# Moving four first loads to ScalarE's queue, narrower idle products, ScalarE for a copy, and a later start of a small task, in a four-layer graph network on one core

## The chip, the cores and the metric

The kernel runs on one core of a Trainium2 chip. The core has TensorE (PE in the profile; its weight loads are shown as PEld), VectorE (DVE), ScalarE (ACT), GpSimd (POOL) and SyncE (SP). SyncE issues nearly all transfers from memory. A queue carries out its instructions in order, so an instruction that waits holds all behind it. The metric is the device time of one execution in microseconds (us), as the median of several runs.

## The reference

The input is x, 3327 nodes by 64 features, and adj, a weighted and nearly empty 3327 by 3327 adjacency matrix. Four layers follow one another, each on a layer-normalised input clipped at zero, and each added to x:

```
h = max(layernorm(x), 0)
layer 0: two gated cells:  m = adj @ (h @ W);  h = relu(GRU(m, h))     # x += h
layer 1: w = decayed weights by the rank of a nonzero among the last 100 of its row
         x += w @ (h @ weight) + bias
layer 2: three hops with adj*adj:  h = (adj*adj @ h) @ W.T + b         # x += h
layer 3: two hops:  h = tanh(concat[adj @ h, h] @ W[k])                # x += h
```

In one cell, `r = sigmoid(i_r + h_r)`, `z = sigmoid(i_z + h_z)`, `n = tanh(i_n + r*h_n)` and the new h is `(1-z)*n + z*h`, where the three i come from m and the three h from the old h. So adj is multiplied eight times by a 64-column matrix, and everything else is small beside that.

## The kernel before

**Tiling.** The nodes are padded to 26 blocks of 128, laid out as 13 pairs of blocks. The 13 pairs form four chunks of 3, 3, 3 and 4 pairs (384, 384, 384 and 512 columns for each of the two halves), and two groups: group 0 holds chunks 0 and 1, group 1 chunks 2 and 3. A tile is one block of 128 sources against all columns of one group: 768 KB for group 0 and 896 KB for group 1. Tiles live in 20 slots. `Tile.load` (line 409) takes the slot that has been free longest and issues the transfer on SyncE's queue (line 412).

**Products.** There are eight products with adj, k = 0 to 7: 0 and 1 are the two cells, 2 is the ranked layer, 3 to 5 are the squared hops, 6 and 7 the last layer. `alone` and `joint` (lines 646 and 662) write a list of units (k, chunk, tile). A `joint` stage uses each tile for two products, k and k+1, one group at a time, so that the tile is loaded once. Beside product 0 a counting product (line 549) is made of a 0/1 mask of each tile, which VectorE writes (line 473). It gives the number of nonzeros behind each block, kept in `totals`. In product 2, masks (line 473 on 127 rows, the last row brought by a GpSimd transfer of `totals`, line 478) are multiplied by a triangle of constants (called from line 517, shown under line 314), and ScalarE or VectorE turn the sums into the bits of a weight e (lines 530 and 528). Then TensorE multiplies e by the features (line 614).

**Order of the work.** The order on every engine is fixed when the program is written: `run` (line 718) walks the list of units, up to 44 units ahead with loads, 24 with masks and 3 with the expansion to e. All other work stands in tasks, which are Python generators. A task yields a number of planned microseconds. `spend` (line 381) takes a planned price for each unit from every task's number and lets those tasks go on whose number has run out. `later_task(us, task)` starts a task after so many planned microseconds from the start of `run`. `finish` makes a task go to its end where its result is needed.

**What is touched.**

- `load_x` (line 118) and lines 1043 to 1051: before `run`, x is loaded in three parts and four tiles between them, all on SyncE's queue: x part 0, tile, x part 1, tile, tile, rest of x, tile. `load_cell(0)` then loads the first cell's weights and all biases (lines 154 and 157) into `stage`, which GpSimd has set to zero before (line 1043).
- `warm_up` (line 172) makes 14 products (28 instructions) of x with itself that nobody reads, 384 columns each, ahead of the first true product.
- `before_0` makes the layer norm of a chunk (lines 841 to 856), whose result y is the first product's input, and transposes it (line 798; copies at line 800).
- `evacuate_stacked` (line 830) copies a product's sums out: the upper half on ScalarE (line 831), the lower half on VectorE (line 832). `gru` (line 872) calls it for both cells and goes on with the gates (line 883), the sigmoids (line 888), two VectorE steps (lines 893 and 895), tanh (line 904) and the blend (lines 908 to 915).
- `last_sources(g)` (line 565) prepares the last row of every block as sources of the ranked layer, as one extra unit: GpSimd clears half a slot (line 571), SyncE loads two small parts (line 575), VectorE makes two steps (lines 577 and 581) and ScalarE one (line 583). Its result `lastw` is used by the last unit of each chunk in product 2. For group 0 it starts at planned time 130, for group 1 at 155 (line 1062).

Of the kernel before, what the change touches and what calls it, by code (L numbers as in the profile page):

```python
# [44 lines left out]
N, D = 3327, 64  # L45
P = 128
NB = 13
# [4 lines left out]
CH = [(0, 3), (3, 6), (6, 9), (9, 13), (3, 5), (5, 6)]  # L52
NC = 4
# [11 lines left out]
W1, IH1, HH1, W2, IH2, HH2 = 0, 1, 4, 7, 8, 11  # L65
# [26 lines left out]
def upper(n):  # L92
    return slice(n * D, (n + 1) * D)
# [3 lines left out]
def kernel(  # L97
# [9 lines left out]
    nc = tc.nc  # L107
# [7 lines left out]


    xs = const.tile([P, NB, 2, D], F32, name="xs")
    def load_x(g0, g1):
        nc.sync.dma_start(out=xs[:, g0:g1], in_=x[:, g0:g1])

    load_x(*CH[0])
    slots = [const.tile([P, 2, GWM], F32, name=f"adj{i}") for i in range(NBUF)]
    mhalf = const.tile([P, 8], F32, name="mhalf")
    nc.gpsimd.memset(mhalf, -0.5)
# [3 lines left out]
    stage = const.tile([P, 7 * D + NBIAS], F32, name="stage")  # L128
    w3 = const.tile([P, 2, 2, D], F32, name="w3")
    both = [const.tile([P, 2, (b1 - b0) * P], F32, name=f"both{c}") for c, (b0, b1) in enumerate(CH[:NC])]  # L130
# [20 lines left out]
                            compare_op=ALU.is_gt, fill=0.0, base=2 - P, channel_multiplier=1)  # L151

    def load_cell(cell):
        nc.sync.dma_start(out=stage[upper(0), :7 * D].rearrange("p (w f) -> p w f", f=D),
                          in_=weights[:, (W1, W2)[cell]:(W1, W2)[cell] + 7])
        if cell == 0:
            nc.sync.dma_start(out=stage[upper(0), 7 * D:], in_=bias_cols)

    def unfold_cell(cell):

# [11 lines left out]
    def warm_up():  # L172

        i, ps = take()
        for n in range(7):
            for h in range(2):
                nc.tensor.matmul(ps[upper(h), :width(0)], xs[:, 0, h, :], flat(xchunk(0)), start=True, stop=True)
        give(i)

    def fold_cell(cell):  # L180
# [67 lines left out]
    def more_constants():  # L248
# [32 lines left out]
        for c in range(NC):  # L281
            yield 4.0
            ahead_of_cell(c)
        yield 47.0
        load_cell(1)
        yield 20.0
        unfold_cell(1)
# [15 lines left out]
    def blocks(c):  # L303
        return CH[c][1] - CH[c][0]

    def width(c):
        return blocks(c) * P
# [15 lines left out]
    def take(sums=False, either=True):  # L323


        either = either and not sums
        pool = idle_sums if sums else idle_temps
        if either and idle_sums and (not pool or released[idle_sums[0]] < released[pool[0]]):
            pool = idle_sums
        for c in list(tasks):  # L330
            if not pool and c not in running:
                advance(c)
        i = pool.popleft()
        return i, banks[i]

    def give(i):
        released[i] = max(released) + 1
        (idle_sums if i < 4 else idle_temps).append(i)
# [5 lines left out]
    def flat(t):  # L344
        return t.rearrange("p b s d -> p b (s d)")
# [4 lines left out]
    def xchunk(c):  # L350
        return xs[:, CH[c][0]:CH[c][1]]
# [8 lines left out]
    def advance(c):  # L360
        running.add(c)
        try:
            tasks[c][1] = next(tasks[c][0])
        except StopIteration:
            del tasks[c]
        running.discard(c)

    def begin(c, task):
        finish(c)
        tasks[c] = [task, 0.0]  # L370
        advance(c)

    def finish(c):
        while c in tasks:
            advance(c)

    def later_task(us, task):
        yield us
        yield from task
# [185 lines left out]
    def last_sources(g):  # L565

        w = sum(width(c) for c in GROUPS[g])
        w0 = CH[GROUPS[g][0]][0] * P
        room = Mask(w)
        v = room.view.rearrange("p s w -> p (s w)").bitcast(F32)  # L570
        nc.gpsimd.memset(v, 0.0)  # L571
        yield 4.0
        rows = adjT.rearrange("(q p) (s n) -> q p s n", p=P, s=2)
        for s in range(2):
            nc.sync.dma_start(out=v[s * D:s * D + NQ], in_=rows[:, P - 1, s, w0:w0 + w])
        yield 12.0
        nc.vector.tensor_scalar(v, v, 0.0, 129.0 * TWO7, op0=ALU.not_equal, op1=ALU.mult)
        for c in GROUPS[g]:
            finish(("count", c))
        yield 1.0  # L580
        nc.vector.scalar_tensor_tensor(v, totals[g], -TWO7, v, op0=ALU.mult, op1=ALU.add)
        yield 1.5
        nc.scalar.activation(lastw[g], v, AF.Relu, bias=bitsb)
        room.free()
# [37 lines left out]
    units = []  # L622
# [204 lines left out]
                yield 1.2  # L827
        return yk

    def evacuate_stacked(acc, c):  # L830
        nc.scalar.copy(both[c][upper(0), 0], acc[0][1][upper(0), :width(c)])  # L831
        nc.vector.tensor_copy(both[c][upper(1), 1], acc[1][1][upper(1), :width(c)])  # L832
        for i in {acc[0][0], acc[1][0]}:
            give(i)

# [36 lines left out]
    def gru(acc, c, bi, bh, cell, pace=1.0):  # L872

        w = width(c)
        evacuate_stacked(acc, c)
        yield 0.8 * pace
        at = dead.popleft()
        r, z, d = (slots[at].rearrange("p s w -> p (s w)")[:, i * CWM:i * CWM + w] for i in range(3))

        def gate(g):  # L880
            i, ps = take()
            for s in range(2):
                nc.tensor.matmul(ps[upper(1 - s), :w], cells[:, cell, s, g, :], both[c][:, s], start=True, stop=True)
            return i, ps

        for g, v in enumerate((r, z)):
            i, ps = gate(g)
            nc.scalar.activation(v, ps[:, :w], AF.Sigmoid, bias=bsum[:, cell, g:g + 1])
            give(i)
        nh = None if cell == 0 else gate(2)  # L890
        ni = gate(3)
        yield 1.0 * pace
        nc.vector.scalar_tensor_tensor(r, ahead[c] if nh is None else nh[1][:, :w], bcol[:, bh + 2:bh + 3], r,
                                       op0=ALU.add, op1=ALU.mult)
        nc.vector.tensor_tensor(r, r, ni[1][:, :w], ALU.add)
        give(ni[0])
        if nh is not None:
            give(nh[0])
        else:
            del ahead[c]  # L900
            if not any(ch in ahead for ch in GROUPS[c // 2]):
                rooms[c // 2].free()
        yield 1.0 * pace
        nc.scalar.activation(r, r, AF.Tanh, bias=bcol[:, bi + 2:bi + 3])
        yield 0.8 * pace
        for s in range(2):
            u = upper(1 - s)
            nc.vector.tensor_tensor(d[u], both[c][u, s], r[u], ALU.subtract)
        nc.vector.tensor_tensor(d, d, z, ALU.mult)
        nc.vector.tensor_tensor(d, d, r, ALU.add)  # L910
        if cell == 0:
            nc.vector.tensor_scalar(both[c][upper(0), 1], d[upper(0)], 0.0, None, op0=ALU.max)
        yield 2.4 * pace
        if cell == 0:
            nc.scalar.activation(both[c][upper(1), 0], d[upper(1)], AF.Relu)
            yield 1.0 * pace
        return at, d
# [27 lines left out]
    def after_0(c, acc):  # L945
        at, _ = yield from gru(acc, c, BI1, BH1, 0)
        dead.append(at)
        i, v = stacked_to_nodes(c, lambda s: ident[:, upper(1 - s)])
        yield 0.8
        yk = nodes(c)  # L950
        nc.vector.tensor_copy(flat(yk), v)
        give(i)
        y[1][c] = yk

    def after_1(c, acc):
        pace = 1.0 if c in GROUPS[0] else 1.2
        at, h2T = yield from gru(acc, c, BI2, BH2, 1, pace)
        v = transpose_to_nodes(h2T, c)
        dead.append(at)
        yield 0.8 * pace  # L960
        residual(v, c, relu=True)
        yk = nodes(c)
        yield from layernorm_relu(yk, c, TWO27, 1.2 * pace, squares_on_scalar=c in GROUPS[1])
        y[2][c] = yield from in_three(yk, c)
        yield 80.0 if c in GROUPS[1] else 14.0
        add_row(c, 3)
# [40 lines left out]
    def after_6(c, acc):  # L1007
        evacuate_stacked(acc, c)
        yield 1.3
        v = stacked_to_nodes(c, lambda s: w3[:, 0, s])  # L1010
        yk = nodes(c)
        nc.scalar.activation(flat(yk), v[1], AF.Tanh)
        give(v[0])
        y[7][c] = yk
        yield 8.0
        yield from transpose_on_vector(yk, c)
# [24 lines left out]
    alone(0, 7, sweep=6, parts=True)  # L1041

    nc.gpsimd.memset(stage, 0.0)
    first = list(dict.fromkeys(t for _, _, t in units))[:4]
    first[0].load()
    load_x(*CH[1])
    first[1].load()
    first[2].load()
    load_x(CH[2][0], NB)
    first[3].load()  # L1050
    load_cell(0)
    warm_up()
    for c in (0, 0, 0, 1, 0, 1, 1):
        if c in tasks:
# [4 lines left out]
    begin(2, later_task(4.0, before_0(2)))  # L1059
    begin(3, later_task(10.0, before_0(3)))  # L1060
    begin(NC + 1, later_task(130.0, last_sources(0)))
    begin(NC + 2, later_task(155.0, last_sources(1)))
    run()
    for c in list(tasks):
        finish(c)
# [39 lines left out]
```

## Time and profile before

| | us |
|---|---|
| median of 3 runs (703.73 to 704.52) | 703.85 |
| the profiled execution's own time | 704.14 |
| its span, first to last instruction | 702.2 |
| busy: TensorE | 684.9 |
| busy: weight loads, beside TensorE's products | 378.0 |
| busy: VectorE | 348.8 |
| busy: ScalarE | 271.9 |
| busy: GpSimd | 80.5 |

201 MB are moved, 287 GB/s over the span. A line of the timeline gives start, duration, engine, line of the kernel, operation, output and inputs with their shape, and, where an engine had stood before, how long and for whom in brackets. Products in four-byte numbers appear as two instructions each.

### The profile page before, as it was taken

The numbers are of one execution on the slowest core, as the hardware profiler recorded it, in microseconds if no ns is written. First come the engines' busy times: TensorE is split into PE (matmuls) and PEld (weight loads), VectorE is DVE, ScalarE is ACT, GpSimd is POOL, SyncE is SP. The second block draws the span as 40 slices with busy tenths as digits, with TensorE's granted clock in tenths as the row PEclk, the third lists the DMA queues.
The fourth block names the chain that finished last, engine by engine and source line by source line (L and its number), as shares of the span: only waits on it lengthen the run. The fifth ranks groups of instructions, "written<-read, shape, count | busy, mean of one in ns | idle before, by whom it ended". The sixth has DMA issues, their size and how long they took to land.

```text
span 702.2 us, 12670 instructions
## 1 busy us (share of the span) xinstructions
PE 684.9 (98%) x5128; PEld 378.0 (54%) x5128; DVE 348.8 (50%) x746; ACT 271.9 (39%) x422; POOL 80.5 (11%) x114
## 2 busy tenths in 40 slices
PE   7998999999999999999999999999999999999997
PEld 3684667744566686446444444333444444344586
DVE  4945835733997889747533106425271565005101
ACT  1112100212146878888998206832166600000101
POOL 5300000002284233011100000000000000000000
PEclk9999999999999999999999999999999999999999
DMA  8999998089776943683799659963998399917991
GB/s 312 401 402 404 406 406 278 1 295 401 252 240 257 385 162 101 235 290 100 268 386 347 237 179 408 405 250 122 385 366 270 107 398 405 406 73 273 403 403 49
DMA packets 68693, 201.31 MB, mean 287 GB/s; under 512 B 7244, under 2 KB 8372, under 8 KB 68636
## 3 DMA queue, kind: packets, MB, share of 16 engines
q1 hardware_dynamic: 65740, 199.46, 76.3%
q8 instruction: 40, 0.66, 0.4%
q10 hardware_dynamic: 720, 0.85, 0.3%
q0 software_dynamic: 2176, 0.20, 0.2%
q14 instruction: 17, 0.14, 0.1%
HBM read 199.45 MB, written 0.85 MB: 285 GB/s over the span
## 4 chain that ended last, share of the span: by engine, by line
PE 58%; DVE 1%; ACT 0%; POOL 0%; issue 0%; ACTq 0%; DVEq 0%; POOLq 0%
PE sum L614 54%; PE temp L314 3%; PE temp L781 1%; POOL st L852 0%; DVE xs L1026 0%; ACT t L1023 0%; DVE both L832 0%; ACT both L831 0%; DVE e L528 0%; ACTq L1028 0%; PE sum L314 0%; DVE y L848 0%; DVE t L843 0%; DVE y L856 0%; DVE st L849 0%
## 5 line engine op out<-in xcount | busy, mean ns | idle before, releaser
L614 PE MATMUL sum<-adj,y 128*64 128x384 f32 (+3 forms) x3016 | 535.8, 501 | 3.7 <-DMA adj<-in_adjT 2.5
L614 PEld LDWEIGHTS sum<-adj,y 128*64 128x64 f32 x3016 | 247.0, 137 | 233.8 <-issue 193.9
L447 ACT ACTIVATE adj<-adj 128x768 f32<-128x768 f32 (+1 forms) x176 | 144.2, 891 | 45.2 <-PE sum L614 22.8
L473 DVE TENSOR_SCALAR adj<-adj 128x768 bf16<-128x768 f32 (+3 forms) x208 | 113.5, 597 | 32.6 <-PE temp L549 24.7
L614 PE MATMUL sum<-e,both 128*64 128x384 bf16 (+1 forms) x624 | 73.9, 339 | 0.5 <-DVE e L528 0.5
L530 ACT ACTIVATE e<-temp,bitsb 128x384 int16<-128x384 f32 (+1 forms) x120 | 67.5, 608 | 14.4 <-PE temp L314 8.1
L831 ACT COPY both<-sum 64x384 f32<-64x384 f32 (+3 forms) x17 | 8.1, 478 | 151.2 <-PE sum L614 150.1
L832 DVE COPY both<-sum 64x384 f32<-64x384 f32 (+3 forms) x17 | 9.6, 568 | 109.7 <-ACT both L831 109.7
L852 POOL TENSOR_TENSOR st<-st,mhalf 128x6 f32<-128x6 f32 (+1 forms) x16 | 24.8, 1553 | 288.3 <-DVE st L850 288.3
L449 DVE TENSOR_TENSOR adj<-adj 128x768 f32<-128x768 f32 (+1 forms) x32 | 30.6, 1005 | 52.0 <-DMA adj<-in_adjT 33.3
L314 PE MATMUL temp<-adj,tri 128*64 128x384 bf16 (+1 forms) x332 | 51.4, 341 | 1.3 <-DVE e L528 1.2
L614 PEld LDWEIGHTS <-both 128*64 128x64 bf16 x624 | 41.2, 110 | 19.0 <-issue 6.5
L528 DVE TENSOR_SCALAR e<-temp 128x384 int16<-128x384 f32 (+1 forms) x46 | 28.3, 617 | 20.8 <-ACT e L530 10.9
L314 PEld LDWEIGHTS <-tri 128*64 128x64 bf16 x416 | 28.9, 110 | 17.4 <-issue 9.0
L478 POOL DMA_DIRECT2D adj<-totals x52 | 31.5, 607 | 51.6 <-PE temp L314 44.6
L810 DVE STREAM_TRANSPOSE both<-y 32x96 f32<-32x96 f32 (+1 forms) x128 | 35.6, 278 | 2.9
L549 PE MATMUL temp<-adj,behind 128*64 128x384 bf16 x208 | 33.7, 340 | 2.8 <-DVE adj L473 2.8
L826 DVE STREAM_TRANSPOSE y<-t 32x96 f32<-32x96 f32 (+1 forms) x64 | 17.8, 278 | 25.4 <-ACT t L817 24.5
L549 PEld LDWEIGHTS <-behind 128*64 128x64 bf16 x208 | 20.3, 110 | 16.6 <-issue 13.0
L762 DVE COPY t<-sum 128x384 f32<-128x384 f32 x6 | 3.3, 555 | 34.9 <-PE sum L614 34.9
L187 ACT COPY t<-temp 128x128 f32<-128x128 f32 x1 | 0.3, 266 | 48.2 <-PE temp L185 48.2
L571 POOL MEMSET adj<- 128x768 f32 (+1 forms) x2 | 1.9, 950 | 137.6 <-PE sum L614 137.6
(130 smaller groups left out, 353.3 us busy)
## 6 DMA issues: line engine op xcount, KB each, us to landing
adj<-in_adjT SPq DMA_DIRECT2D x130, 768.0 KB, 8.9
adj<-in_adjT SPq DMA_DIRECT2D x104, 896.0 KB, 12.1
xs<-in_x SPq DMA_DIRECT2D x1, 448.0 KB
adj<-totals POOLq DMA_DIRECT2D x26, 3.0 KB, 5.0
adj<-totals POOLq DMA_DIRECT2D x26, 3.5 KB, 3.2
xs<-in_x SPq DMA_DIRECT2D x2, 192.0 KB, 2.5
out<-xs ACTq DMA_DIRECT2D x2, 192.0 KB
out<-xs ACTq DMA_DIRECT2D x1, 256.0 KB
```

The lines of the kernel that those rows point to most:

```text
L314: nc.tensor.matmul(out[hs], lhsT[:, hs], rhs, start=start, stop=stop)
L447: nc.scalar.activation(sq, v, AF.Square)
L449: nc.vector.tensor_tensor(sq, v, v, ALU.mult)
L473: nc.vector.tensor_scalar(t.mask.view[:rows, half], t.view()[:rows, half], 0.0, None, op0=ALU.not_equal)
L478: nc.gpsimd.dma_start(out=t.mask.view[P - 1:P], in_=totals[t.g][t.q:t.q + D + 1:D, :])
L528: nc.vector.tensor_scalar(wide[:, s], ps[:, :w], BITS, 0.0, op0=ALU.add, op1=ALU.max)
L530: nc.scalar.activation(wide[:, s], ps[:, :w], AF.Relu, bias=bitsb)
L549: nc.tensor.matmul(counts[c][1][s * D:(s + 1) * D, :w], behind[:, NQ - 1 - t.q:NQ - 1 - t.q + D], t.mask.view[:, s, t.cols(c)], start=firs ...
L614: nc.tensor.matmul(acc[h][1][h * D:(h + 1) * D, :w], yq[h], rhs[h], start=first and n == 0, stop=last and n == len(terms) - 1)
L810: nc.vector.transpose(to[at:at + 32, :, q], h[q * 32:(q + 1) * 32, :, s, f * 32:(f + 1) * 32])
L826: nc.vector.transpose(yk[q * 32:(q + 1) * 32, :, s, f * 32:(f + 1) * 32], v[at:at + 32, :, q])
L852: nc.gpsimd.tensor_tensor(st[:, 3, :n], st[:, 2, :n], mhalf[:, :n], ALU.pow)
```

## The change

The rest of x, and the first cell's weights and the biases, are issued on ScalarE's queue; the four tiles are no longer loaded ahead of `run`, which loads them first thing. The idle products have 192 columns. In the first cell, both copies of the sums are ScalarE's. Group 1's last sources start at planned time 200.

```diff
-    def load_x(g0, g1):
-        nc.sync.dma_start(out=xs[:, g0:g1], in_=x[:, g0:g1])
-
-    load_x(*CH[0])
+    for queue, (g0, g1) in ((nc.sync, CH[0]), (nc.scalar, CH[1]), (nc.scalar, (CH[2][0], NB))):
+        queue.dma_start(out=xs[:, g0:g1], in_=x[:, g0:g1])
...
     def load_cell(cell):
-        nc.sync.dma_start(out=stage[upper(0), :7 * D].rearrange("p (w f) -> p w f", f=D),
-                          in_=weights[:, (W1, W2)[cell]:(W1, W2)[cell] + 7])
+        queue = nc.sync if cell else nc.scalar
+        queue.dma_start(out=stage[upper(0), :7 * D].rearrange("p (w f) -> p w f", f=D),
+                        in_=weights[:, (W1, W2)[cell]:(W1, W2)[cell] + 7])
         if cell == 0:
-            nc.sync.dma_start(out=stage[upper(0), 7 * D:], in_=bias_cols)
+            queue.dma_start(out=stage[upper(0), 7 * D:], in_=bias_cols)
...
-                nc.tensor.matmul(ps[upper(h), :width(0)], xs[:, 0, h, :], flat(xchunk(0)), start=True, stop=True)
+                nc.tensor.matmul(ps[upper(h), :3 * D], xs[:, 0, h, :], xs[:, 0:3, 0], start=True, stop=True)
...
-    def evacuate_stacked(acc, c):
+    def evacuate_stacked(acc, c, on_scalar=False):
         nc.scalar.copy(both[c][upper(0), 0], acc[0][1][upper(0), :width(c)])
-        nc.vector.tensor_copy(both[c][upper(1), 1], acc[1][1][upper(1), :width(c)])
+        if on_scalar:
+            nc.scalar.copy(both[c][upper(1), 1], acc[1][1][upper(1), :width(c)])
+        else:
+            nc.vector.tensor_copy(both[c][upper(1), 1], acc[1][1][upper(1), :width(c)])
...
-        evacuate_stacked(acc, c)
+        evacuate_stacked(acc, c, on_scalar=cell == 0)
...
     nc.gpsimd.memset(stage, 0.0)
-    first = list(dict.fromkeys(t for _, _, t in units))[:4]
-    first[0].load()
-    load_x(*CH[1])
-    first[1].load()
-    first[2].load()
-    load_x(CH[2][0], NB)
-    first[3].load()
     load_cell(0)
...
-    begin(NC + 2, later_task(155.0, last_sources(1)))
+    begin(NC + 2, later_task(200.0, last_sources(1)))
```

## The prediction

> **What bounds the kernel now.** I read the page's totals, then the half-microsecond windows of the start, then the order of time around every place where TensorE (PE) stands.
>
> ```profile
> PE 684.9 (98%) x5128; PEld 378.0 (54%) x5128; DVE 348.8 (50%) x746; ACT 271.9 (39%) x422; POOL 80.5 (11%) x114
> ```
>
> PE is busy 684.9 of 702.2 us, so only its 17.3 idle us can be won. By windows they lie in 0 to 40 us (3.4 before the first product, then 1.6, 1.0 and 0.3), 40 to 60 (0.5), 60 to 80 (2.2), 220 to 240 (1.6), 260 to 300 (1.4), and at the end, which the change doesn't touch.
>
> The start, in windows of 0.5 us; columns: stretch, length, busy of PE, PEld, DVE, ACT, POOL, clock, DMA share, GB/s:
>
> ```profile
> 2.00:2.50 0.50, 0.00 (x0) 0.00 (x0) 0.00 (x0) 0.09 (x1) 0.40 (x1) 1.00 0.78 221
> 2.50:3.00 0.50, 0.00 (x0) 0.00 (x0) 0.00 (x0) 0.00 (x0) 0.00 (x0) 1.00 0.78 151
> 3.00:3.50 0.50, 0.14 (x2) 0.14 (x4) 0.16 (x1) 0.00 (x0) 0.00 (x0) 1.00 0.50 68
> 3.50:4.00 0.50, 0.50 (x2) 0.15 (x4) 0.47 (x2) 0.00 (x0) 0.00 (x0) 1.00 0.66 209
> 4.00:4.50 0.50, 0.50 (x4) 0.24 (x2) 0.47 (x2) 0.00 (x0) 0.00 (x0) 1.00 0.98 393
> ```
>
> From 4 us the DMA engines are full, at 390 to 406 GB/s, until after 100 us; before that there is a hole. In the first stage PE needs 1.6 us for a tile (8 products of 0.16, 4 counting ones of 0.08) and a 786 KB tile takes 1.94 us, so PE, late at first, catches up at 54.9 us and then waits for tiles. The last one lets it go at 60.77. Timeline from there; columns: start, length, engine, line, what, idle before:
>
> ```profile
> 60.77 0.87 PE L614 MATMUL sum<-adj,y 128*64 128x384 f32 x4 [0.75 <-DMA adj<-in_adjT]
> ...
> 65.65 0.47 ACT L831 COPY both<-sum 64x384 f32<-64x384 f32 x1 [0.72 <-PE sum L614]
> 66.16 0.56 DVE L832 COPY both<-sum 64x384 f32<-64x384 f32 x1 [1.88 <-ACT both L831]
> 66.75 0.56 DVE L473 TENSOR_SCALAR adj<-adj 128x768 bf16<-128x768 f32 x1
> 67.22 0.61 DVE L893 SCALAR_TENSOR_TENSOR adj<-adj,bcol,adj 128x384 f32<-128x384 f32 x1
> 67.36 0.32 PE L549 MATMUL temp<-adj,behind 128*64 128x384 bf16 x1 [0.95 <-DVE adj L473]
> ```
>
> VectorE stands 1.88 us at L832 because ScalarE copies first; the mask L473 is queued behind it, and PE waits 0.95 us for that mask. From 80 us on PE is the bound, so what is won earlier stays won. VectorE then holds PE twice; first where group 1's last sources are prepared now (VectorE, then PE):
>
> ```profile
> 230.48 0.55 DVE L528 TENSOR_SCALAR e<-sum 128x384 int16<-128x384 f32 x1
> 230.95 1.08 DVE L581 SCALAR_TENSOR_TENSOR adj<-totals,adj 128x896 f32<-128x896 bf16 x1
> 231.95 0.55 DVE L848 TENSOR_TENSOR y<-t 128x384 f32<-128x384 f32 x1
> 232.53 0.55 DVE L849 TENSOR_REDUCE st<-y 128x6 f32<-128x384 f32 x1
> 233.12 0.17 DVE L850 TENSOR_SCALAR st<-st 128x6 f32<-128x6 f32 x1
> 233.20 0.56 DVE L528 TENSOR_SCALAR e<-temp 128x384 int16<-128x384 f32 x1
> ```
>
> ```profile
> 233.81 0.82 PE L314 MATMUL temp<-adj,tri 128*64 128x384 bf16 x4 [0.91 <-DVE e L528]
> ```
>
> PE waits 0.91 us for an L528 that has L581 ahead of it. And second, where they would go (PE, then VectorE):
>
> ```profile
> 280.62 0.65 PE L614 MATMUL sum<-e,both 128*64 128x384 bf16 x5 [0.46 <-DVE e L528]
> ```
>
> ```profile
> 280.03 0.54 DVE L528 TENSOR_SCALAR e<-temp 128x384 int16<-128x384 f32 x1
> 280.50 0.61 DVE L473 TENSOR_SCALAR adj<-adj 127x896 bf16<-127x896 f32 x1
> 281.03 0.68 DVE L528 TENSOR_SCALAR e<-sum 128x512 int16<-128x512 f32 x1
> ```
>
> VectorE has no gap between 262 and 285 us, and PE uses each e as soon as it is written.
>
> **What the Trainium skill says.** "DMA: Bandwidth & Descriptors", section "Issuing engines are not separate DMA queues": transfers started by ScalarE and SyncE run on the same 16 engines and only the issue time is saved. Section "Queues, rings and completion order" adds that each engine goes round between the queues packet by packet, so x and the first tile will share. No transfer of before is on ScalarE's queue at the start, so the trace can't confirm it; the hole shows what issue time can be worth. "TensorE: Matmul & The Clock Gate", part 1: full clock after about 3.4 us of activity, half again after an idle window as long. The trace agrees roughly: pairs of idle products start 0.64 us apart until 6.5 us, 3.1 us after the first, then 0.32. "ScalarE: Activation LUTs", "What ACT_TABLE_LOAD costs": some 1.28 us; the trace has 1.28.
>
> **The change, part by part.**
>
> *Loads.* Four issues leave SyncE's queue between the tiles (0.59, 0.70, 0.64, 0.95 us) and four go to ScalarE's, where only a table load and, from 12.9 us, the copies L800 stand behind. Weights and bias wait there for the memset of stage, done at 2.4 us; delayed table load: free, 1.28 us must fit before 12.9, and four issues of 2.9 us after 0.8 end near 4. The bytes ahead of the last tile stay the same, so only the hole counts. Between 2 and 4 us 324 KB moved; at the 402 GB/s of the next us it would be 805, a lack of 481 KB or 1.2 us. The 640 KB of x now issued from 0.8 us can fill part, but the first x transfer, alike in shape, got at most 221 GB/s. I take 0.8 us won; ends 0.2 lost (x's first part arrives later by sharing) and 1.2 won. VectorE's reduction of chunk 1, which stood 1.47 us for x at 7.54 with chunk 0's last step behind it, runs at once, and y is ready near 8.1 instead of 9.4. That alone wins nothing: PE then stands longer for tile 3, at 15.75 now behind the same bytes.
>
> *Idle products.* 28 instructions, 6.28 us, with 192 for 384 columns: half the time each, ending near 7.4. Nothing, since y at 8.1 covers it; if the clock fell, the clock rival pays.
>
> *Copies of cell 0.* Chunk 0: two copies on ScalarE take 0.97 us (L800's pair), from 61.68 to 62.65, against 62.75 now: 0.1. The table load for sigmoid behind them shifts 0.48 us, the first sigmoid from 63.70 to 63.95; PE has group 1's products meanwhile. Chunk 1: the mask runs by 64.3, PE goes on at 66.41, then the gates need both copies, 65.55 + 0.97 = 66.5; they began at 67.37, so 0.75 won; with waits of 0.25 (74.61) and 0.20 (79.47) on masks perhaps eased, 0.9 in all. Ends 0.3 (the next mask late instead) and 1.5. Chunks 2 and 3: VectorE's waits of 9.54 and 1.18 us go, but PE idles only 0.3 us between 180 and 200: 0.1.
>
> *Group 1's last sources.* One memset on POOL (1.16 us), two transfers on SyncE (0.73), L577 (0.62) and L581 (1.08) on VectorE, L583 (1.04) on ScalarE. Adding the planner's charges unit by unit, 155 falls just before ranked layer 2 of group 0 (memset 213.56, L581 230.95); 200 falls two units before that layer's last sources of chunk 0 (260.5), with L577 just ahead of the L528 at 281.03, L581 two masks later and L583 near 285. On SyncE the transfers now hold the queue 8.8 us for the memset, and POOL's mask rows stand behind it, yet PE hardly waits for either; at the new place POOL is idle from 260.7 to 268.75 and the next tile load is near 280, so both cost nothing. If the memset came later than 280 it would hold tiles. Taken away: the 0.91 wait at 233.81 and most of the 0.29 at 231.08: 1.1 won (ends 0.3, 1.2). Added: L577 pushes e straight onto PE, 0.55; L581 delays the e after 283.23 by 1.6 in all, of which about 1 us of lead and the gaps VectorE has after 285 (0.38, 0.46, 1.16) take most: 0.35. Lost 0.9 (ends 0.4 and 4.5: 1.7 on VectorE, 1.04 and a wait of 1.25 as at 232.06 on ScalarE, and 0.5 of squares behind). Net 0.2 won.
>
> Sum: 0.8 + 0.9 + 0.1 + 0.2 = 2.0 us. Profiled span 702.2 to 700.2, its own time 704.14 to 702.1; against the median of 703.85, which lies 0.3 below the profiled run, **701.8**.
>
> **Rivals.** *The stream isn't earlier* (0.22): descriptors of both queues compete and the hole stays; for it speaks that x's small rows moved at 0.78 share with 221 GB/s. Then 1.2 is left: 702.6. *VectorE is full at the new place* (0.15): L577 and L581 reach PE whole, 1.7 plus 0.4; net 1.0 lost instead of 0.2 won: 703.0; the gaps after 285 speak against it. *The clock falls* (0.06): idle products end at 7.4, then tiles come by drops; half rate for one window of 3.4 us loses 1.7, of which PE's standing before tile 3 takes half: 702.7. *Slower* (0.12): L583, in ScalarE's queue, holds e and the squares of layer 3 behind it while it waits for L581, as it did 1.25 us at 232; the whole 4.5 us reaches PE: 703.85 - 0.8 - 1.0 - 1.1 + 4.5 = 705.4. It decides from 2.9 us on; ScalarE is 80% busy between 280 and 300. That the copies win nothing belongs to the first rival's size.
>
> **How the numbers follow.** My forecast has 0.45. 0.2%, about what a measurement of this kernel can tell from none, is 1.4 us: faster ends at 702.4. Forecast 0.40 of its 0.45 below that, the first rival 0.08, the others 0.04: faster 0.52. Slower, above 705.3: 0.07 of the last rival's 0.12 and 0.03 from causes I have not seen, 0.10. The rest, 0.38, is same. Best ends of all parts: 1.2 + 1.5 + 0.2 + 0.8 = 3.7, so 700.1; at the top, the last rival's lower half, 704.9, holds 8 in 10.
>
> **What would show it.** DMA near 300 GB/s or more between 2.5 and 4 us; the last tile's product before 60.2; no wait of VectorE at the copies of cell 0; chunk 1's gates 5.9 us after the last tile's first product (6.6 now); no PE wait over 0.3 us in the stage of ranked layer 2, group 0, where 231 to 234 now is; a wait of about 0.5 to 1 us more near 281 to 286. I am wrong if the first tile products begin earlier but the last tile lands at 60.7 as before, or if ScalarE stands at L583 with PE idle.

## The result and the profile after

The changed kernel takes **700.36 us** (median of 4 runs, 700.23 to 700.46), against 703.82 for the kernel before beside it (4 runs, 703.73 to 704.52): a ratio of 0.9949, with a 95% interval of 0.9931 to 0.9966. Forecast were 701.8 in a range of 700.1 to 704.9. So the direction was right, and the gain was 3.5 us where 2.0 were forecast. The profiled execution took 700.41 us, with a span of 698.6. Some lines have other numbers in the new kernel: L314, L473, L528, L549, L577, L581, L614 and L883 of before are L313, L472, L527, L548, L576, L580, L613 and L885 there; the copies are L830 and, now ScalarE's, L832.

The totals of the page after:

```profile
PE 682.1 (98%) x5128; PEld 379.7 (54%) x5128; DVE 347.1 (50%) x742; ACT 274.4 (39%) x426; POOL 78.6 (11%) x114
```

PE has the same 5128 instructions and is busy 2.8 us less, 1.9 of it in the idle products (6.28 before, 4.37 now). Its idle time is 698.6 - 682.1 = 16.5 us, against 17.3 before. Busy and idle totals hide the change here; only places do. The start of the changed kernel, in the same windows and columns as before:

```profile
2.00:2.50 0.50, 0.00 (x0) 0.00 (x0) 0.00 (x0) 0.00 (x0) 0.40 (x1) 1.00 0.56 74
2.50:3.00 0.50, 0.00 (x0) 0.00 (x0) 0.00 (x0) 0.00 (x0) 0.00 (x0) 1.00 0.98 313
3.00:3.50 0.50, 0.00 (x0) 0.00 (x0) 0.00 (x0) 0.00 (x0) 0.00 (x0) 1.00 0.94 328
3.50:4.00 0.50, 0.00 (x0) 0.00 (x0) 0.00 (x0) 0.00 (x0) 0.00 (x0) 1.00 1.08 429
4.00:4.50 0.50, 0.38 (x3) 0.29 (x5) 0.40 (x1) 0.00 (x0) 0.00 (x0) 1.00 1.01 413
```

The hole is filled: between 2.5 and 4 us the DMA engines move 313 to 429 GB/s, where they moved 68 to 209. PE starts 0.8 us later, because x's first part lands later: the first product starts at 3.2 to 3.4 us in the five traces with the old loads and at 3.9 to 4.5 us in the nine with the new. But the true products begin earlier, because y is ready sooner. PE from the timeline after:

```profile
4.12 4.37 PE L176 MATMUL temp<-xs 128*64 128x192 f32 x28 [4.12 <-DMA xs<-in_x]
...
8.92 1.51 PE L613 MATMUL sum<-adj,y 128*64 128x384 f32 x8 [0.43 <-DVE y L858]
```

The end of the first stage, all engines (before: last tile at 60.77, VectorE standing 1.88 us at its copy, PE 0.95 us at the mask):

```profile
58.33 0.87 PE L613 MATMUL sum<-adj,y 128*64 128x384 f32 x4 [0.25 <-DMA adj<-in_adjT]
...
63.12 0.47 ACT L830 COPY both<-sum 64x384 f32<-64x384 f32 x1 [0.53 <-PE sum L613]
63.43 0.63 DVE L472 TENSOR_SCALAR adj<-adj 128x896 bf16<-128x896 f32 x1
63.61 0.47 ACT L832 COPY both<-sum 64x384 f32<-64x384 f32 x1
63.64 0.19 PEld L885 LDWEIGHTS sum<-both,cells 128*64 128x64 f32 x2
63.64 2.33 PE L885 MATMUL sum<-both,cells 128*64 128x384 f32 x11
```

The last tile lets PE go 2.44 us earlier; the mask runs beside ScalarE's copies instead of behind VectorE's, and chunk 1's gates start at 63.64, when the first copy is written; the first of their products that needs the second copy starts at 64.14. The new place of group 1's last sources, VectorE, then PE:

```profile
275.84 0.62 DVE L576 TENSOR_SCALAR adj<-adj 128x896 f32<-128x896 f32 x1
276.38 0.68 DVE L527 TENSOR_SCALAR e<-sum 128x512 int16<-128x512 f32 x1
276.98 1.15 DVE L472 TENSOR_SCALAR adj<-adj 127x896 bf16<-127x896 f32 x2
278.04 1.08 DVE L580 SCALAR_TENSOR_TENSOR adj<-totals,adj 128x896 f32<-128x896 bf16 x1
279.05 0.62 DVE L472 TENSOR_SCALAR adj<-adj 127x896 bf16<-127x896 f32 x1
279.58 0.55 DVE L527 TENSOR_SCALAR e<-sum 128x384 int16<-128x384 f32 x1
280.05 0.68 DVE L527 TENSOR_SCALAR e<-temp 128x512 int16<-128x512 f32 x1
```

```profile
277.11 0.81 PE L613 MATMUL sum<-e,both 128*64 128x512 bf16 x5 [0.61 <-DVE e L527]
...
280.19 1.08 PE L613 MATMUL sum<-adj,y 128*64 128x512 f32 x4 [1.19 <-DVE e L527]
```

L576 pushes one e, L580 the next two, and PE stands 0.61 and 1.19 us.

The ledger of a kernel with one bound engine is best kept by instruction: I took the start of the same PE instruction in both traces, and the difference is what has been won by then. Negative is earlier than in the trace of before; the first column is the time there.

| before, us | what starts | after |
|---|---|---|
| 9.47 | first product of a tile | -0.55 |
| 16.45 | after tile 3 | -1.89 |
| 54.89 | PE has caught up with the tiles | -1.29 |
| 60.77 | last tile of stage one | -2.44 |
| 67.75 | gates of chunk 1 | -3.61 |
| 138.11 | second cell | -3.56 |
| 178.25 | | -3.86 |
| 236.13 | behind the old place of last sources | -5.18 |
| 280.95 | ahead of the new place | -5.18 |
| 283.83 to 697.79 | behind it, to the end | -3.64 |

### The profile page after: what moved, and what is told of

Same layout as the page of the kernel before. It is cut to its first block, busy times and chain, and to the rows that moved or that the text cites. A ratio compares the mean times of both kernels' runs of the same rounds, so it can differ in the third digit from the quotient of the medians.

```text
span 698.6 us, 12663 instructions
## 1 busy us (share of the span) xinstructions
PE 682.1 (98%) x5128; PEld 379.7 (54%) x5128; DVE 347.1 (50%) x742; ACT 274.4 (39%) x426; POOL 78.6 (11%) x114
## 4 chain that ended last, share of the span: by engine, by line
PE 87%; DVE 7%; DMA 3%; POOL 2%; issue 1%; ACT 1%; ACTq 0%; DVEq 0%; POOLq 0%
PE sum L613 74%; PE temp L313 5%; DMA adj<-in_adjT 2%; PE temp L548 2%; PE temp L885 2%; DVE adj L472 2%; PE sum L313 1%; PE sum L885 1%; PE temp L780 1%; DVE e L527 1%; POOL both L251 1%; POOL st L854 1%; DVE st L851 1%; DVE adj L910 1%; DMA xs<-in_x 0%
## 5 line engine op out<-in xcount | busy, mean ns | idle before, releaser
L613 PE MATMUL sum<-adj,y 128*64 128x384 f32 (+3 forms) x3016 | 535.7, 501 | 2.8 <-DVE e L527 1.2
L613 PEld LDWEIGHTS sum<-adj,y 128*64 128x64 f32 x3016 | 247.5, 137 | 231.9 <-issue 198.2
L472 DVE TENSOR_SCALAR adj<-adj 128x768 bf16<-128x768 f32 (+3 forms) x208 | 113.5, 596 | 32.6 <-PE temp L548 24.7
L613 PE MATMUL sum<-e,both 128*64 128x384 bf16 (+1 forms) x624 | 73.9, 339 | 1.0 <-DVE e L527 1.0
L830 ACT COPY both<-sum 64x384 f32<-64x384 f32 (+3 forms) x17 | 8.1, 478 | 149.1 <-PE sum L613 148.0
L834 DVE COPY both<-sum 64x384 f32<-64x384 f32 (+3 forms) x13 | 7.2, 560 | 102.6 <-ACT both L830 102.6
L613 PEld LDWEIGHTS <-both 128*64 128x64 bf16 x624 | 41.2, 110 | 19.6 <-issue 7.0
L313 PE MATMUL temp<-adj,tri 128*64 128x384 bf16 (+1 forms) x332 | 51.4, 341 | 0.4 <-DVE e L527 0.2
L477 POOL DMA_DIRECT2D adj<-totals x52 | 34.4, 662 | 46.2 <-PE temp L313 32.4
L527 DVE TENSOR_SCALAR e<-temp 128x384 int16<-128x384 f32 (+1 forms) x46 | 28.3, 617 | 20.6 <-ACT e L529 10.9
L313 PEld LDWEIGHTS <-tri 128*64 128x64 bf16 x416 | 28.9, 110 | 16.1 <-issue 7.8
L548 PE MATMUL temp<-adj,behind 128*64 128x384 bf16 x208 | 33.8, 340 | 2.8 <-DVE adj L472 2.6
L548 PEld LDWEIGHTS <-behind 128*64 128x64 bf16 x208 | 20.8, 110 | 17.3 <-issue 13.5
```

The lines of the kernel that those rows point to most:

```text
L313: nc.tensor.matmul(out[hs], lhsT[:, hs], rhs, start=start, stop=stop)
L472: nc.vector.tensor_scalar(t.mask.view[:rows, half], t.view()[:rows, half], 0.0, None, op0=ALU.not_equal)
L477: nc.gpsimd.dma_start(out=t.mask.view[P - 1:P], in_=totals[t.g][t.q:t.q + D + 1:D, :])
L527: nc.vector.tensor_scalar(wide[:, s], ps[:, :w], BITS, 0.0, op0=ALU.add, op1=ALU.max)
L548: nc.tensor.matmul(counts[c][1][s * D:(s + 1) * D, :w], behind[:, NQ - 1 - t.q:NQ - 1 - t.q + D], t.mask.view[:, s, t.cols(c)], start=firs ...
L613: nc.tensor.matmul(acc[h][1][h * D:(h + 1) * D, :w], yq[h], rhs[h], start=first and n == 0, stop=last and n == len(terms) - 1)
```

## The experiments

Times are medians, with the ratio to runs of the kernel before on the same chip. Traces are read with the ledger above, always against the same trace of before.

**One part at a time, and the idle products put back.** The first run makes only the loads' part, the idle products staying at 384 columns:

```diff
+    for queue, (g0, g1) in ((nc.sync, CH[0]), (nc.scalar, CH[1]), (nc.scalar, (CH[2][0], NB))):
+        queue.dma_start(out=xs[:, g0:g1], in_=x[:, g0:g1])
...
+        queue = nc.sync if cell else nc.scalar
...
-    first = list(dict.fromkeys(t for _, _, t in units))[:4]
...
-    first[3].load()
```

> The kernel before with the loads alone: rest of x, first weights and biases on ScalarE's queue, tiles in SyncE's queue at once. Theory A (bytes and uneven engines: the landings of a tile on the 16 DMA engines lie 0.6 us apart after the change and 1.8 us before, and the last tile is ready 2.4 us earlier): the last tile of the first stage lands near 58.3 us, but with the long idle products the first product comes near 10.5 us and TensorE becomes the later of the two; the median falls by 1.5 to 2.4 us. Theory B (what I predicted: only the hole before 4 us is filled): last tile near 59.7 to 60, median 0.8 to 1.1 us lower. Theory C (the shorter idle products are what counts): less than 0.5 us.

The second makes only the copies' part:

```diff
-        evacuate_stacked(acc, c)
+        evacuate_stacked(acc, c, on_scalar=cell == 0)
```

> The kernel before with both copies of the first cell on ScalarE, nothing else. Theory A (my prediction: VectorE's wait of 1.88 us and with it TensorE's of 0.95 us go): median 0.7 to 1.1 us lower, gates of chunk 1 at about 66.6 instead of 67.4 us. Rival (the win of the changed kernel at this place came only because the tiles were earlier): 0.3 us or less. A second rival from the later stages (the changed kernel also gains 0.6 us between 80 and 190 us, where chunks 2 and 3 go through the same cell): then 1.3 to 1.7 us.

The third only moves the last sources:

```diff
-    begin(NC + 2, later_task(155.0, last_sources(1)))
+    begin(NC + 2, later_task(200.0, last_sources(1)))
```

> The kernel before with group 1's last sources started at 200 instead of 155, nothing else. Theory A (from the two traces: 1.0 us won where they were, 1.5 us lost where they go): median 0.3 to 0.7 us higher. Theory B (my prediction): 0.2 us lower. Theory C (the new place only costs because the other edits made VectorE busier there): 0.5 us lower or more.

The fourth is the changed kernel with long idle products:

```diff
-                nc.tensor.matmul(ps[upper(h), :3 * D], xs[:, 0, h, :], xs[:, 0:3, 0], start=True, stop=True)
+                nc.tensor.matmul(ps[upper(h), :width(0)], xs[:, 0, h, :], flat(xchunk(0)), start=True, stop=True)
```

> The changed kernel with the long idle products (384 columns) put back. Theory A (they became the thing that holds the first product, since x's first part lands 0.75 us later): first tile product near 10.5 instead of 8.9 us, the catching-up of TensorE with the tiles is not reached, and the median is 0.3 to 1.3 us above the changed kernel's. Theory B (my prediction: their length is covered): equal to the changed kernel within 0.2 us.

| | median us (lowest to highest) | ratio, 95% | last tile | 138 | 178 | 217 | 236 | end |
|---|---|---|---|---|---|---|---|---|
| before | 704.13 (702.59 to 705.76) | | | | | | | |
| loads alone | 702.67 (702.18 to 703.34) | 0.9981, 0.9975 to 0.9988 | -2.07 | -2.00 | -2.30 | -1.21 | -1.21 | -1.26 |
| copies alone | 702.50 (701.19 to 703.75) | 0.9974, 0.9967 to 0.9981 | -1.31 | -2.43 | -2.72 | -1.47 | -1.48 | -1.52 |
| move alone | 703.04 (702.66 to 704.63) | 0.9988, 0.9979 to 0.9997 | -1.14 | -1.15 | -1.13 | -1.14 | -2.47 | -0.97 |
| all, long idle products | 700.76 (700.54 to 701.57) | 0.9953, 0.9936 to 0.9970 | -1.44 | -2.50 | -2.79 | -2.80 | -4.14 | -2.62 |

Each part wins by itself. The loads' 1.5 us lie between Theories A and B. The copies' 1.6 have the size of their second rival, but by the trace 1.1 of it had come by 138 us, and the 0.3 at 172 to 178 us isn't theirs, since the loads alone have it too. The move's 1.1 have the size of Theory C, but not its reason: PE still loses 1.54 us at the new place (-2.51 ahead of it, -0.97 behind). The three medians' gains add up to 4.2 us, more than the whole change brings; the piece of 0.3 is counted twice in that, and the rest is within what the intervals allow.

Two columns were in none of my theories. First, the copies and the move can't touch the start of the kernel, and still their last tile came 1.1 to 1.3 us earlier than in the trace of before. Second, the loads alone and the copies alone lose 1.1 and 1.25 us between 178 and 217 us, where neither part has anything to do, and the kernels with the move don't. Both became questions for the next runs.

The long idle products end at 12.17 us in the last kernel, when y has been ready since 9.24, and at 11.26 us in the loads alone, which has them too (y since 8.90). In both the last tile finds PE late, by 1.28 and 0.58 us after its landing, and no wait for a tile is left there. So that part wasn't worth nothing.

**The loss at 200 to 215 us.** In the trace of the copies alone, VectorE, GpSimd, and PE:

```profile
203.20 7.62 DVE L473 TENSOR_SCALAR adj<-adj 127x768 bf16<-127x768 f32 x13
210.84 0.56 DVE L835 COPY both<-sum 64x384 f32<-64x384 f32 x1
```

```profile
203.57 2.23 POOL L938 DMA_DIRECT2D lasty<-both  x4 [1.74 <-DVE both L931]
205.79 0.86 POOL L571 MEMSET adj<- 128x896 f32 x1
206.58 5.51 POOL L478 DMA_DIRECT2D adj<-totals  x7
```

```profile
211.46 1.18 PE L886 MATMUL temp<-both,cells 128*64 128x384 f32 x5 [0.80 <-DVE both L835]
```

Thirteen masks take 7.62 us where the same thirteen took 6.19 before. One of them alone takes 1.95 us instead of 0.55:

```profile
205.12 1.95 DVE L473 TENSOR_SCALAR adj<-adj 127x768 bf16<-127x768 f32 x1
```

It is the one beside GpSimd's memset at 205.79, which clears the slot for group 1's last sources. Copy L835 is queued behind the masks, and PE waits 0.80 us for it. In the trace of before, the memset came late:

```profile
206.13 7.43 POOL L935 DMA_DIRECT2D lasty<-both  x4 [0.74 <-DVE both L928]
213.56 1.16 POOL L571 MEMSET adj<- 128x896 f32 x1
```

There one of GpSimd's own transfers took 5.90 us to issue, and the memset fell on a mask (1.28 us, at 213.85) that held nobody. The Trainium skill, "SBUF — State Buffer", section "SBUF: two separate sides", says that a VectorE operation in a two-port mode and a GpSimd operation use one port pair as an exclusive lock, and that the later one blocks until the first has finished. The traces agree that the two hinder each other. Where the memset starts first it is the mask that waits, as the page has it: in the changed kernel's new place the memset starts at 253.93, and a mask 0.14 us later takes 1.17 us instead of 0.62 (no loss for PE there). But in the copies alone the mask is recorded from 205.12, before the memset, and still it is the mask that grew, by 1.40 us, beside a memset of 0.86. To test whether the memset is the cause, the copies' part was run again with the clearing on VectorE itself:

```diff
-        nc.gpsimd.memset(v, 0.0)
+        nc.vector.memset(v, 0.0)
```

> The kernel with only the copies of the first cell on ScalarE, group 1's last sources at 155, and their half slots cleared by VectorE instead of GpSimd. Theory A (GpSimd's clearing falls into a run of masks on VectorE and stretches one of them from 0.55 to 1.95 us, and TensorE then waits 0.80 us at 211 us for the copy behind it): no mask over 0.7 us near 205, the wait at 211 us gone or under 0.3, and the median 0.5 to 1.2 us below the copies alone (702.5). Theory B (the long mask has another cause): the long mask and the wait stay, median within 0.3 us of 702.5.

VectorE in that run:

```profile
203.07 2.00 DVE L473 TENSOR_SCALAR adj<-adj 127x768 bf16<-127x768 f32 x4
205.21 0.81 DVE L571 MEMSET adj<- 128x896 f32 x1
205.93 4.23 DVE L473 TENSOR_SCALAR adj<-adj 127x768 bf16<-127x768 f32 x9
210.20 0.56 DVE L835 COPY both<-sum 64x384 f32<-64x384 f32 x1
```

The thirteen masks take 6.23 us again and PE's wait falls from 0.80 to 0.11 us; between 178 and 217 us 0.56 is lost instead of 1.25, and VectorE's own 0.81 us of clearing, ahead of the same copy, is enough for that. The median is 702.19 (701.80 to 702.96; ratio 0.9974, 0.9962 to 0.9986). That is 0.3 under the copies alone, where Theory A had 0.5 to 1.2, and the ratio to the kernel before is the same: the mechanism is shown by the trace, its size in the time is not.

**The place of the last sources.** Two runs move only the number in the changed kernel, to 170 and to 220:

```diff
-    begin(NC + 2, later_task(200.0, last_sources(1)))
+    begin(NC + 2, later_task(170.0, last_sources(1)))
```

> The changed kernel with group 1's last sources started at 170 instead of 200, so that VectorE's two steps fall near 240 to 247 us, where it stands 0.25 us in every 0.8 for TensorE. Theory A (their cost is VectorE's fullness at the place where they fall): the 1.5 us lost near 281 us come back, and little is lost near 245: 0.8 to 1.5 us below the changed kernel, 698.9 to 699.6. Theory B (ScalarE's step and its wait, wherever they fall, cost as much): within 0.3 us of the changed kernel.

> The changed kernel with group 1's last sources started at 220, so that VectorE's steps fall near 290 us, where it has gaps of 0.4 to 1.2 us and ScalarE is 80% busy. Theory A (VectorE's fullness): the 1.5 us near 281 mostly gone, 0.5 to 1.5 us below the changed kernel. Theory B (ScalarE's step in its full queue): 1 us or more above it. In either case GpSimd's clearing falls into masks of VectorE near 280 us and may cost up to 1.4 us there.

With them ran the changed kernel itself, unedited:

> The changed kernel once more, as the yardstick for the first two on the same chip, and for how far the landings of the first tiles on the 16 DMA engines differ from one execution to another. If the uneven engines belong to the program: 2.0 to 2.1 us between first and last engine at the last tile of the first stage, as in its first trace; if they are chance: anything between 1.8 and 3.4.

| | median us (lowest to highest) | ratio, 95% | 236 | 281 | 284 | end |
|---|---|---|---|---|---|---|
| before | 704.20 (703.30 to 704.79) | | | | | |
| start 170 | 698.62 (698.55 to 698.75) | 0.9922, 0.9905 to 0.9938 | -5.53 | -5.54 | -5.54 | -5.55 |
| start 200 (the change) | 700.19 (700.04 to 701.00) | 0.9946, 0.9931 to 0.9961 | -4.72 | -4.72 | -3.19 | -3.19 |
| start 220 | 699.69 (699.49 to 699.89) | 0.9936, 0.9922 to 0.9951 | -5.54 | -5.55 | -5.05 | -4.47 |

With 170 the old place's gain is kept, and nothing is lost later. VectorE there:

```profile
239.94 0.55 DVE L527 TENSOR_SCALAR e<-sum 128x384 int16<-128x384 f32 x1
240.41 0.62 DVE L576 TENSOR_SCALAR adj<-adj 128x896 f32<-128x896 f32 x1
240.94 1.01 DVE L527 TENSOR_SCALAR e<-temp 128x384 int16<-128x384 f32 x2
241.87 1.08 DVE L580 SCALAR_TENSOR_TENSOR adj<-totals,adj 128x896 f32<-128x896 bf16 x1
```

VectorE stood 0.80 us twice shortly before, at 237.17 and 239.00. In the changed kernel it also stands four times 0.25 us for PE between 242 and 245 us, and these waits are gone with 170: VectorE was ahead of PE, and the two steps push no e that PE is waiting for. PE's waits for e show the three places side by side (total, times, longest); start 200, then 170, then 220:

```profile
PE sum L613 <- DVE e L527: 2.2, 3, 1.2
```

```profile
PE sum L613 <- DVE e L527: 0.6, 2, 0.5
```

```profile
PE sum L613 <- DVE e L527: 1.2, 3, 0.6
...
PE sum L613 <- ACT e L529: 0.4, 1, 0.4
```

At 220 the loss is smaller but comes in two pieces, 0.50 near 281 us and 0.56 further on, the second where PE waits 0.39 us for an e of ScalarE. The first piece is again GpSimd's clearing, which starts at 274.71 there; the mask beside it with 220, then the same mask with 170:

```profile
274.94 1.12 DVE L472 TENSOR_SCALAR adj<-adj 127x896 bf16<-127x896 f32 x1
```

```profile
274.95 0.61 DVE L472 TENSOR_SCALAR adj<-adj 127x896 bf16<-127x896 f32 x1
```

The e behind that mask is 0.49 us later, and PE waits 0.58 us for it. The version with 170 beats both kernels: 698.62, which is 1.6 under the changed kernel beside it. Its gain is one number in one line.

**The arrival of the last tile.** Is the 1.0 to 1.3 us by which last tiles came earlier without cause chance? The kernel before was profiled again, unedited:

> The kernel before once more, one look. Theory A (chance has a part: which of the 16 DMA engines an instruction fetch of 16 KB meets, and whether GpSimd's clearing comes late): the last tile of the first stage lands near 59.5 us rather than 60.7, 1.9 to 2.4 us after the first engine has its part instead of 3.4, and GpSimd's clearing stretches a mask near 206 us and TensorE waits 0.6 to 0.8 us near 211 us, as in the single edits that keep the start at 155. Theory B (both belong to the program): 60.7 us, 3.4 us and no wait near 211 us, as in its first trace.

Its PE at the last tile, and at 213 us:

```profile
59.76 0.87 PE L614 MATMUL sum<-adj,y 128*64 128x384 f32 x4 [0.76 <-DMA adj<-in_adjT]
...
213.14 1.18 PE L883 MATMUL temp<-both,cells 128*64 128x384 f32 x5 [0.73 <-DVE both L832]
```

The same kernel starts its last tile 1.01 us earlier than its first trace has it, loses 1.19 us at 205 to 213 through the stretched mask, and ends 0.19 later. The first trace of before was unusual twice, in opposite directions, with nearly the usual sum.

Why does a tile come when it does? By the Trainium skill, "DMA: Bandwidth & Descriptors", section "Why a DMA increments its semaphore by 16 and not by 1", a transfer runs on up to 16 engines that finish independently, and only the last of them lets the reader go. The trace records each engine's completion. For the last tile of stage one, in us of each span:

| | first engine | last engine | between |
|---|---|---|---|
| loads as before: first trace | 57.33 | 60.73 | 3.40 |
| the same, again | 57.34 | 59.72 | 2.38 |
| copies alone; move alone; copies with VectorE's clearing | 57.52; 57.22; 57.17 | 59.42; 59.58; 59.46 | 1.90; 2.36; 2.29 |
| loads as changed: first trace | 56.24 | 58.29 | 2.05 |
| the same, again | 56.19 | 58.78 | 2.59 |
| loads alone; all, long idle products; start 170; start 220 | 56.29; 56.10; 56.10; 56.03 | 58.12; 58.05; 57.94; 57.96 | 1.83; 1.95; 1.84; 1.93 |

The first engine depends on the kernel alone, within 0.35 us: 57.2 to 57.5 with the old loads, 56.0 to 56.3 with the new, so about 1.1 us earlier. The lag of the last engine, 1.8 to 3.4 us here, depends on the execution.

Not all of the 1.1 us comes from the hole before 4 us. Two longer stretches of the start, before and then after (the last number is GB/s):

```profile
0.00:4.50 4.50, 1.14 (x4) 0.53 (x6) 1.09 (x3) 1.28 (x1) 1.59 (x11) 1.00 0.44 122
4.50:15.00 10.50, 9.67 (x62) 4.12 (x58) 7.35 (x15) 0.95 (x2) 5.52 (x7) 1.00 1.02 374
```

```profile
0.00:4.50 4.50, 0.38 (x3) 0.29 (x5) 0.40 (x1) 0.00 (x0) 1.60 (x11) 1.00 0.57 177
4.50:15.00 10.50, 9.87 (x77) 5.81 (x74) 8.27 (x17) 2.23 (x3) 6.03 (x7) 1.00 1.03 394
```

The five traces with the old loads have 115 to 122 GB/s and then 372 to 376, the seven with the changed loads (the changed kernel's third trace, below, among them) 177 to 197 and then 388 to 394. At 402 GB/s the mean differences are worth 0.8 us by 4.5 us and 0.4 us more by 15 us; from there to 55 us the rates are alike, 399 to 401. What makes the second stretch faster was not tested.

Or do the small rows of the weights, now ahead of the tiles, even the engines out? In this run they went back to SyncE's queue, behind four tiles:

```diff
-        queue = nc.sync if cell else nc.scalar
+        queue = nc.sync
...
+    for t in list(dict.fromkeys(t for _, _, t in units))[:4]:
+        t.load()
```

> The changed kernel with the first cell's weights and the biases back on SyncE's queue, behind the first four tiles; x stays on ScalarE's. Theory A (x fills the hole before 4 us; the weights only change place): the first engine has its part of the last tile of the first stage at 56.0 to 56.3 us as in the changed kernel, time within 0.5 us of it. Theory B (the weights' 64 short rows in the tiles' queue are what makes the engines uneven): the first engine at 56.2 us, but the last 3 us or more behind it.

A single profiled run gave 702.24 us, with 56.26 for the first engine, 59.97 for the last, and 3.71 between them. That left it open, so it was timed, beside the changed kernel once more:

> The changed kernel, but with the first cell's weights and the biases on SyncE's queue again, behind the first four tiles; only the two later parts of x go through ScalarE. The single look at this kernel took 702.24 us, with 3.71 us between the first and the last of the 16 engines at the last tile of stage one, but its engines lay 2.1 us apart already before the weights' turn. A (chance: the weights don't matter, engines differ from run to run): median within 0.5 us of the changed kernel beside it, about 700.2, and the spread of the profiled run anywhere between 1.8 and 3.7. B (64-row weights behind the tiles make some engines late): median near 702, and a spread above 3 us again.

> The changed kernel itself, on the same chip as the run with the weights on SyncE's queue. Both theories: 700.2 to 700.5 us as before; it is the measure for that run.

Weights on SyncE's queue: 700.50 us (700.23 to 700.78), 56.27 to 58.67, so 2.40 between the engines. The changed kernel: 700.37 (700.20 to 700.47), 56.29 to 58.37, so 2.08. The large lag was chance: the medians differ by 0.13 us, the ranges overlap, and one execution can be 1.7 us off. What makes one engine late in one execution and not in another I can't say.

## Why the prediction was right, and where it was not

*Which term.* By the first two traces the start gave 2.44 us, the copies 1.1 and the move -0.2, and that division is partly chance. Over all traces, the last tile starts on average 0.95 earlier than in the first trace of before with the old loads (5 traces, 0 to 1.31), and 2.16 earlier with the new loads and short idle products (7 traces, 0.75 to 2.79, the two with the weights on SyncE's queue among them). So a typical sum, an estimate from these means, is: loads and idle products 1.2, copies 1.1, a piece of 0.3 at 172 to 178 us, the move 0.9; together 3.5, the measured 3.46. In the forecast stood 0.8, 1.0, nothing and 0.2. The measured time lies just inside the range, 0.3 us above its lower end, at which every part wins its most.

*Loads: mechanism right, one reading wrong.* The hole was filled, and by 4.5 us that is worth the 0.8 us that I took, although the reason for taking no more, x's small rows at 221 GB/s, didn't hold: the engines moved 313 GB/s from 2.5 us on. Wrong was "From 4 us the DMA engines are full, at 390 to 406 GB/s", and with it "only the hole counts". In the trace of before the engines moved 364 GB/s from 12 to 14 us and 334 from 14 to 16, and between 4.5 and 15 us the new loads won another 0.4 us, which the sum had at nothing. The rival that the stream isn't earlier is refuted by the first engine. My sign, the last tile's product before 60.2, could not have decided it: with the old loads it came at 59.5 to 59.8 in four traces of five.

*Idle products: the step failed.* "Nothing, since y at 8.1 covers it" asked only whether the shorter ones end in time, not what the long ones would do once y is early: they hold PE from 9.2 to 12.2 us in one trace and from 8.9 to 11.3 in the other. At the last tile that is 0.7 and 0.1 us (-1.44 and -2.07 against the mean of -2.16), by the medians 0.4 (700.76 against 700.36). The execution with 0.7 was the slowest of its four, 701.57. Nor did "half the time each" hold: they took 4.37 us and not 3.1, since nearly all pairs started 0.32 us apart, where 0.16 is full pace for 192 columns. The long ones had been at half pace for 3.2 us in the trace of before, but for 3.8 to 6.2 us in six others. y itself came at 8.9 and not 8.1, as x's first part landed 0.8 us later. The clock rival didn't occur: the true products behind y start 0.32 us apart, as before. The clock column doesn't tell this; it shows 1.00 at half pace too.

*Copies: right.* VectorE no longer stands at cell 0's copies. Chunk 1's gates start 5.31 us after the last tile's first product (6.60 before), and with the second copy 5.81 (5.9 forecast). By 138 us the copies alone had won 2.43 - 1.31 = 1.1; 1.0 stood in the sum. The 0.3 at 172 to 178 us isn't theirs. Every kernel that is 1.87 us or more ahead at 172 has it, and none that is 1.2 or less; the cause wasn't found.

*The move: the balance had the right sign by luck, with two errors against each other.* The old place gave 1.33 (1.1 forecast, ends 0.3 and 1.2): both waits went whole. The new place cost 1.54, not 0.9. For L576 PE waits 0.61 us, close to the 0.55 that was forecast. Wrong was "L581 delays the e after 283.23 by 1.6 in all, of which about 1 us of lead and the gaps VectorE has after 285 take most: 0.35". VectorE is busy 19.61 of the 20 us from 260 to 280 in the new trace, and PE waits 1.19 us for the e behind L580, where it waited 0.19 before. The gaps lay behind the e that PE needed, so they covered nothing. And wrong was that the rest "cost nothing": I saw the memset on GpSimd as GpSimd's time only. At its old time it usually stretches a VectorE mask and costs 1.1 to 1.25 us (three traces of four with its old start and GpSimd's clearing: loads alone, copies alone, before again). Moved, it still stretches a mask, but none that PE waits behind. The trace that I predicted from was the fourth, the exception: its sign was a 5.90 us issue among four of one kind, which I read over. So typically the move won 1.33 + 1.1 - 1.54 = 0.9, as it did alone in the time (1.1 by the medians).

*Rivals.* L583 on ScalarE, which was to decide the slower case, held PE nowhere in the changed kernel; PE's only wait for ScalarE's e appears at 220, 0.39 us. The rival of a full VectorE was right about the place, 1.54 lost where it had 2.1, and wrong about the sum.

## What to carry to other kernels

Ask of every small step on the bound engine's feeders where the feeder is ahead: VectorE had stood twice for 0.80 us just before 240 us, and there two steps of 1.7 us cost nothing, while 36 us later they cost 1.5. When one edit makes a result earlier, cost the work beside it anew in its old form; that is where the idle products' worth lay. A small step on an engine that isn't the bound one can still hold it through a third: GpSimd's clearing reached TensorE through a VectorE mask. And profile the kernel before twice ahead of arguing from a wait below a microsecond or so: two events of chance of 1.0 and 1.2 us stood in this one trace.

## What the runs showed of the hardware that I had not expected

- The last of the 16 engines came 1.8 to 3.7 us after the first at one 768 KB tile, and the lag differs between executions of one kernel (3.40 and 2.38; 2.05, 2.59 and 2.08). The tile is as late as that engine.
- A GpSimd memset of 0.86 us beside a run of VectorE masks from four-byte to two-byte numbers made one mask 1.95 us instead of 0.55 in three traces, which is more than the memset takes. The clearing on VectorE takes 0.81 us and stretches nothing.
- In the first trace of before the memset came late, and both sides were slower: it took 1.16 us, and the three masks at 212.91 took 2.22 instead of 1.50.
- TensorE's first products run at half pace (pairs 0.64 us apart, then 0.32) for 3.2 to 6.2 us in the seven traces with idle products of 384 columns, while the profile's clock column shows 1.00.
